# Graph layer with edge sums on one core: the last four groups counted in advance, and their first places sent through DRAM as a 123rd row of the rank product

## Chip, core and metric

The kernel runs on 1 core of one Trainium2 chip. The metric is the device time of an execution in microseconds (us); lower is better. Engines are called PE or TensorE (matrix products), DVE or VectorE, ACT or ScalarE, POOL or GpSimd (here it issues the indirect transfers) and SP or SyncE (here it issues nearly all direct transfers).

## What is computed

```python
def _L0_gnn_ref(x, edge_index, edge_features, ...):
    row = edge_index[0]                                   # the source node of each edge
    edge_aggr = jnp.zeros((n, 128)).at[row].add(edge_features)
    combined = jnp.concatenate([x, edge_aggr, global_expand], axis=-1) @ W_c + b_c
    h = jax.nn.softplus(combined @ W1 + b1)
    h = jax.nn.softplus(h @ W2 + b2)
    return h @ W3 + b3
x = _layernorm(x + _L0_gnn_ref(...), axis=-1)
```

There are 6,250 nodes and 206,250 edges, each with 128 float32 features (106 MB). `src` holds the source node of each edge in no order. Nearly all work is in the second line: the features of the edges are added up by source node. The matrix products of the layer that follows are small.

## The kernel before

**Layout.** The edges stand as 1,692 columns of 122 rows (`PN`). Two columns are a *pair*, so there are 846 pairs, which fall into eight *groups* of 28, 72, 124, 124, 124, 128, 124 and 122 pairs. The nodes are cut into 32 *buckets* of 196 (`BL`). The kernel sorts the edges by bucket, through DRAM, and then sums each bucket with matrix products.

**Sorting a pair.** ScalarE or VectorE builds a one-hot of each edge's place in its pair (*compare*: `sort_hot`, L1139 on VectorE, L1142 and L1144 on ScalarE); TensorE multiplies the edges' rows by it (*gather*: `sorted`, L1155); ScalarE copies the sorted rows into one of six buffers (*settle*: `pairs`, L1167); POOL issues one indirect transfer per pair, which writes the rows to their buckets in DRAM (*scatter*: `rows_by`, L1184). Compare, gather and settle are done for three pairs at a time, a piece. Of the pairs, a share of three in five is compared by VectorE.

**Summing.** SP loads chunks of a bucket back (`chunks<-rows_by`, L293, in six buffers), VectorE makes a one-hot of the node within the bucket (*match*: `hot`, L990), TensorE multiplies (*product*: `part`, L1013), VectorE adds the parts up (*add*: `sums_t`, L1036). A chunk may be loaded once enough columns have been scattered that its rows are certainly there. The planner works this out from sizes of buckets and adds the visits to the order. The chunks of the *last column* become certain only after the last scatter. Then the node layers follow. Room that no edge fills has to be zero, so 23 fill transfers (`rows_by<-fill`) write zeros ahead.

**Positions.** Before a group can be sorted, its positions must be known. Per group: `node_codes` (twelve VectorE operations over the whole group, L357 to L393) gives each edge its bucket; then, per set of 16 columns, `count_set` makes a one-hot of the buckets (`pair_ib`, 122 rows by 512, L498) and `counted` multiplies it by ones (L509). Per batch of four sets VectorE keeps the even counts (L520), TensorE turns them into first places of runs by products with triangular matrices (L527), and VectorE stores these (`started`: L534, L536, and a bfloat16 copy `starts_h`, L538) and handles odd counts (`odd_set`, L546 to L551). Scans over the group end the counting pass. A second pass ranks the edges: per set one product of the rank matrix with `pair_ib` (`ranked`, L557), to which four products with an identity add the first places (L559), and VectorE picks the slot of each edge (L576). Then come the pair tables (L727, L742, L753 to L764).

**The order.** The whole order of instructions is written by a planner: every step gets a due time from modelled durations (1.3 us a scatter), the steps are sorted by time and issued, and each engine then runs its instructions in that order as soon as their inputs are there. The steps for later groups' positions are spread evenly over 0.85 of the time of the group that is being scattered. For groups up to `GAP`, both passes are done in the time of the group ahead. From `GAP` = 5 on, groups are *split*: the counting pass is done early, and the second pass, which makes the one-hots again, in the time of the group ahead. Once the counts of all groups are known, room in the buckets is dealt out exactly: groups before `GAP` fill their buckets from the front, groups from `GAP` on from the end. Fills are due ahead of group `GAP`'s first column.

| scattered meanwhile | positions work before the change |
|---|---|
| group 2 | group 3 whole, count of group 5 |
| group 3 | group 4 whole, count of group 6 |
| group 4 | count of group 7, second pass of group 5 |
| groups 5, 6 | second pass of group 6, of group 7 |

Of the kernel before, what the change touches and what calls it, by code (L numbers as in the profile page):

```python
# [18 lines left out]
P = 128  # L19
# [14 lines left out]
GAP = 5  # L34
# [36 lines left out]
APART = 3  # L71
# [32 lines left out]
def tables_of(n_buckets):  # L104
# [31 lines left out]
    t["rank"] = MARK * (k == f) + (f > k)  # L136
# [10 lines left out]
def kernel(  # L147
# [35 lines left out]
    assert 2 * BATCH * STEP + SPAN <= 4 * P and BATCH * STEP // QUAD + SPAN <= P  # L183
# [98 lines left out]
    totals = dram.tile([N + 2, D], F32, name="totals")  # L282

# [35 lines left out]
    with ExitStack() as phase:  # L319
# [25 lines left out]
        rank_h = rank_h[:PN, :PN]  # L345
# [5 lines left out]
        def scratch(name):  # L351
            return per.tile([P, 4 * P], F32, name=name, bufs=1)
# [98 lines left out]
        def positions(g):  # L451
# [22 lines left out]
            def opened():  # L474
                if sets:
                    if not split:
                        opened2()
                    own["odd"] = per.tile([KB, 2, Q_MAX], BF16, name="odd", bufs=1)
                    own["evens"] = per.tile([KB, Q_MAX], BF16, name="evens", bufs=1)
                    own["alone"] = per.tile([KB, Q_MAX], BF16, name="alone", bufs=1)  # L480
                    late, deep = ("_late", G - GAP) if split else ("", 1)
                    own["starts"] = per.tile([KB, 2, Q_MAX], F32, name="starts" + late, bufs=max(2, deep))
                    own["starts_h"] = per.tile([KB, Q_MAX], BF16, name="starts_h" + late, bufs=deep)
                    own["earlier"] = per.tile([KB, 2, Q_MAX], F32, name="earlier" + late, bufs=deep)
# [7 lines left out]
            def count_set(t):  # L492
                n = size(t)
                m = n // QUAD
                ib = pairs_in.tile([PN, STEP // QUAD, SB, QUAD], BF16, name="pair_ib", bufs=5)[:, :m]
                in_set[t] = ib
                cols = pair_block[:, 2 * s0 + t:2 * s0 + t + n].rearrange("p (q c) -> p q c", c=QUAD)
                nc.vector.tensor_tensor(  # L498
                    ib, cols.unsqueeze(2).to_broadcast([PN, m, SB, QUAD]),
                    bucket_at[:PN].unsqueeze(1).to_broadcast([PN, m, SB, QUAD]),  # L500
                    op=ALU.is_equal)

            def counted(ts):
                small = whole(small_bank())
                small_of["counts", ts] = small
                for t in ts:
                    for q in range(per_set(t)):
# [3 lines left out]
                            in_set[t][:, q].rearrange("p b c -> p (b c)"),  # L511
# [11 lines left out]
            def evened(ts):  # L523
                at = quads_of(ts)
                n = at.stop - at.start
                for k, by in enumerate((lower_h, through_h, lower_or_all_h)):
                    nc.tensor.matmul(small_of["counts", ts][:KB, (1 + k) * P:(1 + k) * P + n], by,  # L527
                                     own["evens"][:, at], start=True, stop=True)

            def started(ts):  # L530
                at = quads_of(ts)
                n = at.stop - at.start
                small = small_of["counts", ts][:KB].rearrange("k (a q) -> k a q", a=4)
# [4 lines left out]
                nc.vector.tensor_copy(own["starts_h"][:, at], small[:, 1, :n])  # L538

            def odd_set(ts):  # L540
                at = quads_of(ts)
                n = at.stop - at.start
                small = small_of.pop(("counts", ts))[:KB].rearrange("k (a q) -> k a q", a=4)
# [9 lines left out]
            def ranked(t):  # L553
# [3 lines left out]
                nc.tensor.matmul(pr, rank_h, in_set.pop(t)[:, :, :NB, :], start=True, stop=False)  # L557
# [270 lines left out]
            else:  # L828
# [367 lines left out]
        with tc.manual_schedule(engines={ET.PE, ET.DVE, ET.Activation, ET.SP}):  # L1196
# [111 lines left out]
            ahead_of[G - 1], position_steps = [], {}  # L1308
# [310 lines left out]
```

## Time and profile before

| | before |
|---|---|
| median of 3 runs | 1282.51 us (1279.74 to 1284.93) |
| the profiled execution | 1280.91 us |
| span of its trace | 1279.1 us |
| busy: PE, its weight loads, DVE, ACT, POOL | 1156.0, 1098.4, 1047.0, 913.4, 883.6 us |
| granted TensorE clock, mean | 0.972 |

The span runs from the first to the last recorded instruction; the execution is 1.8 us longer. Rows of the trace give the start in us, the duration in us, the engine, the line in the code, the operation, what is written from what, and the shape of a tile; x4 says that four instructions are taken together; brackets give the idle time ahead of the row and what ended it. Rows with the releaser "issue" waited for nothing that the profile shows. The line numbers are those of the kernel before; in the changed kernel most stand about 25 lines lower (compare L1164, gather L1180, product L1038, add L1061, one-hot L501, SP's transfers L295).

### The profile page before, as it was taken

How to read it: one execution, taken by the hardware profiler on the slowest of the kernel's cores; microseconds unless marked ns; L12 is line 12 of the kernel's file. 1: busy time of each engine (PE TensorE's matmuls, PEld its weight loads, DVE VectorE, ACT ScalarE, POOL GpSimd, SP SyncE). 2: the span in 40 equal slices, each digit the busy share in tenths (PEclk: the TensorE clock that was granted, in tenths of full speed). 3: DMA queues.
4: the chain of work that ended last, by engine and by line, in shares of the span. 5: the costliest groups of instructions: out<-in, count | busy, mean ns of one | idle time of the engine just before them, and what ended most of it. 6: DMA issues, size and time to landing. Idle time of an engine off the chain costs nothing.

```text
span 1279.1 us, 26170 instructions
## 1 busy us (share of the span) xinstructions
PE 1156.0 (90%) x8617; PEld 1098.4 (86%) x8617; DVE 1047.0 (82%) x2289; ACT 913.4 (71%) x2150; POOL 883.6 (69%) x915
## 2 busy tenths in 40 slices
PE   5777898797998899989899999999999999899893
PEld 4677788787998898989899999999999999898772
DVE  7878979986789898899888887789877767687784
ACT  5887877886776688866987878877888888303343
POOL 2777777776777777777777777777777777750334
PEclk9988999998899899999999999999999999999996
DMA  6789999999999989997999999999999999875421
GB/s 242 249 304 357 334 314 306 346 340 334 338 347 331 333 315 336 322 315 266 320 317 312 313 340 329 337 319 332 322 350 335 363 343 355 286 234 144 142 69 54
DMA packets 174635, 381.95 MB, mean 299 GB/s; under 512 B 27546, under 2 KB 118626, under 8 KB 160670
## 3 DMA queue, kind: packets, MB, share of 16 engines
q1 hardware_dynamic: 130751, 260.70, 61.7%
q0 software_dynamic: 41328, 115.65, 23.3%
q10 hardware_dynamic: 2415, 3.85, 0.8%
q8 instruction: 72, 1.18, 0.4%
q14 instruction: 69, 0.57, 0.1%
HBM read 242.47 MB, written 142.20 MB: 301 GB/s over the span
## 4 chain that ended last, share of the span: by engine, by line
PE 62%; DVE 11%; DMA 11%; ACT 6%; issue 5%; POOL 4%; SPq 0%; ACTq 0%; DVEq 0%; POOLq 0%
PE part L1013 37%; PE sorted L1155 20%; DMA rows_by<-pairs,pair 7%; POOL rows_by L1184 4%; ACT pairs L1167 3%; DMA chunks<-rows_by 3%; DVE hot L990 2%; ACT sort_hot L1142 1%; PE small L557 1%; PE small L559 1%; DVE past L727 1%; DVE sort_hot L1139 1%; PE small L1397 1%; PE sorted L1362 1%; DVE slot L576 1%
## 5 line engine op out<-in xcount | busy, mean ns | idle before, releaser
L1184 POOL DMA_INDIRECT rows_by<-pairs,pair x846 | 830.5, 982 | 289.3 <-issue 208.1
L1167 ACT COPY pairs<-sorted 64x387 f32<-64x387 f32 (+2 forms) x1144 | 543.5, 475 | 224.0 <-PE sorted L1155 165.1
L1013 PE MATMUL part<-hot,chunks 128*128 128x196 f32 x3516 | 671.0, 334 | 16.0 <-DVE sums_t L1036 9.0
L1013 PEld LDWEIGHTS part<-hot,chunks 128*128 128x128 f32 x3516 | 577.4, 191 | 25.2 <-DVE sums_t L1036 10.7
L1155 PE MATMUL sorted<-rows,sort_hot 122*128 122x129 f32 x3384 | 489.6, 284 | 36.3 <-ACT pairs L1167 25.3
L1155 PEld LDWEIGHTS sorted<-rows,sort_hot 122*128 122x128 f32 x3384 | 448.9, 196 | 45.7 <-ACT pairs L1167 35.7
L990 DVE TENSOR_TENSOR hot<-chunks,both_ps 128x784 f32<-128x784 f32 (+3 forms) x541 | 427.1, 810 | 11.7 <-DMA chunks<-rows_by 7.7
L1036 DVE TENSOR_TENSOR sums_t<-sums_t,part 128x392 f32<-128x392 f32 (+1 forms) x262 | 143.6, 548 | 115.9 <-PE part L1013 113.0
L1142 ACT ACTIVATE sort_hot<-plain,slot 122x128 f32<-122x128 f32 x684 | 227.9, 392 | 8.8 <-DVE slot L576 5.9
L1139 DVE TENSOR_TENSOR sort_hot<-slot,both_ps 122x768 f32<-122x768 f32 (+2 forms) x172 | 159.6, 928 | 7.7 <-PE sorted L1155 7.4
L1144 ACT ACTIVATE sort_hot<-sort_hot 122x768 f32<-122x768 f32 x114 | 95.9, 841 | 0.2
L1439 POOL TENSOR_SCALAR y<-y,mv,rs 128x128 f32<-128x128 f32 x40 | 31.3, 788 | 91.1 <-DVE rs L1427 90.8
L576 DVE TENSOR_REDUCE slot<-small 122x16 f32<-122x512 f32 (+2 forms) x109 | 72.9, 669 | 16.5 <-PE small L559 16.0
L498 DVE TENSOR_TENSOR pair_ib<-pair_block,plain 122x512 bf16<-122x512 bf16 (+2 forms) x157 | 63.5, 411 | 0.2
L1369 ACT ACTIVATE away<-sorted,z_bias 128x512 f32<-128x512 f32 (+2 forms) x13 | 8.5, 656 | 71.8 <-DMA chunks<-rows_by 46.4
L557 PE MATMUL small<-pair_ib,half 122*122 122x512 bf16 (+2 forms) x109 | 42.6, 391 | 9.9 <-DVE slot L576 9.6
L742 PEld LDWEIGHTS <-past 128*128 128x128 f16 x424 | 24.7, 98 | 22.6 <-DVE past L727 17.8
L742 PE MATMUL small<-jump,past 128*128 128x56 f16 (+3 forms) x424 | 28.8, 188 | 16.3 <-DVE past L727 12.1
L727 DVE TENSOR_TENSOR past<-both_ps,starts 128x512 f16<-128x512 f32 (+1 forms) x61 | 39.7, 666 | 0.2
L559 PEld LDWEIGHTS <-starts_h 128*122 128x122 bf16 x236 | 24.9, 146 | 13.2 <-issue 8.7
L727 DVE TENSOR_TENSOR past<-both_ps,starts_late 128x512 f16<-128x512 f32 (+2 forms) x49 | 32.4, 662 | 0.0
L1116 ACT COPY rows<-pair_i 122x16 f32<-122x16 f32 x106 | 22.3, 211 | 7.8 <-DMA rows<-in_edge 6.9
(161 smaller groups left out, 516.7 us busy)
## 6 DMA issues: line engine op xcount, KB each, us to landing
rows<-in_edge SPq DMA_DIRECT2D x105, 1032.0 KB
chunks<-rows_by SPq DMA_DIRECT2D x362, 136.0 KB
chunks<-rows_by SPq DMA_DIRECT2D x203, 204.0 KB
chunks<-rows_by SPq DMA_DIRECT2D x75, 272.0 KB
rows_by<-pairs,pair POOLq DMA_INDIRECT x846
rows_by<-fill SPq DMA_DIRECT2D x10, 1249.5 KB
rows_by<-fill SPq DMA_DIRECT2D x10, 714.0 KB
chunks<-rows_by SPq DMA_DIRECT2D x13, 408.0 KB
```

Of the source, the lines that this page charges most:

```text
L498: nc.vector.tensor_tensor(ib, cols.unsqueeze(2).to_broadcast([PN, m, SB, QUAD]), bucket_at[:PN].unsqueeze(1).to_broadcast([PN, m, SB, QUAD ...
L576: nc.vector.tensor_reduce(to, of, axis=mybir.AxisListType.X, op=ALU.max)
L727: nc.vector.tensor_tensor(past[:, :, a:b], twice_ps[:KB].unsqueeze(1).unsqueeze(1).to_broadcast([KB, 2, b - a, P // 2]), own["starts"][:, ...
L990: nc.vector.tensor_tensor(hot[:, q - a:q - a + m], chunks[j][:, lo:hi + 1:step, D:W].to_broadcast([P, m, BL]), iota_ps.unsqueeze(1).to_bro ...
L1013: nc.tensor.matmul(part[:, b - base_of[v], :], t[:, place_in(j, q), :D], hot[:, q - a], start=first, stop=last)
L1036: nc.vector.tensor_add(here, here, of)
L1139: return [lambda: nc.vector.tensor_tensor(hot[:PN, :2 * m], slot[:PN, at:at + 2 * m].unsqueeze(2).to_broadcast([PN, 2 * m, P]), slot_ps[:P ...
L1142: return [lambda j=j: nc.scalar.activation(hot[:PN, j], by_slot[:PN], AF.Abs, bias=slot[:PN, at + j:at + j + 1], scale=-1.0) for j in rang ...
L1144: for j in range(2 * m)] + [lambda: nc.scalar.activation(hot[:PN, :2 * m], hot[:PN, :2 * m], AF.Relu, bias=1.0, scale=-1.0)]
L1155: nc.tensor.matmul(out[:, j, :], hot[:PN, at], rows_at[col // LOAD_COLS][:PN, col % LOAD_COLS, :], start=True, stop=True)
L1167: nc.scalar.copy(sets_at[i][64 * n:64 * n + 64, lo:lo + m, h, :W], out[64 * h:64 * h + 64, :m, :])
L1184: s = nc.gpsimd.indirect_dma_start(out=dst, out_offset=bass.IndirectOffsetOnAxis(ap=at, axis=0), in_=rows[:, j].rearrange("p a b -> p (a b ...
```

## The change

`GAP` becomes 4, so that group 4 is split too, and a table says in which group's time each split group is counted: 4 and 5 in group 2's, 6 and 7 in group 3's.

| scattered meanwhile | positions work after the change |
|---|---|
| group 2 | group 3 whole, counts of groups 4 and 5 |
| group 3 | counts of groups 6 and 7, second pass of group 4 |
| group 4 | second pass of group 5 |
| groups 5, 6 | second pass of group 6, of group 7 |

In split groups the four L559 products per set go. The rank matrix gets a 123rd row of ones, and the one-hot tile a 123rd row that holds the first places of the set. For this, a further product per batch gives the first places turned round (a set's positions in rows), VectorE casts them (`starts_rows`, in place of the `starts_h` cast), SP writes them to DRAM (16 transfers in all), and SP reads for each set of the second pass 512 values of them into row 123 of the one-hot (64 transfers of 1 KB). The rank product of a set comes 13 steps after its one-hot and its row's transfer (`ROW_LEAD`), where it was 3.

```diff
-GAP = 5
+GAP, COUNTED_IN = 4, {4: 2, 5: 2, 6: 3, 7: 3}
-APART = 3
+APART, ROW_LEAD = 3, 13
-    t["rank"] = MARK * (k == f) + (f > k)
+    t["rank"] = MARK * (k == f) + (f > k) + (k == PN)
...
+    rows_of = {g: dram.tile([2 * (s1 - s0) // QUAD, KB], BF16, name=f"starts{g}")
+               for g, (s0, s1) in enumerate(groups) if g >= GAP}
...
-                ib = pairs_in.tile([PN, STEP // QUAD, SB, QUAD], BF16, name="pair_ib", bufs=5)[:, :m]
+                ib = pairs_in.tile([PN + 1, STEP // QUAD, SB, QUAD], BF16, name="pair_ib", bufs=5)[:, :m]
...
+                if split:
+                    nc.tensor.matmul(small_of["counts", ts][:n, P:P + KB], own["evens"][:, at],
+                                     lower_h, start=True, stop=True)
...
-                nc.vector.tensor_copy(own["starts_h"][:, at], small[:, 1, :n])
+                if not split:
+                    nc.vector.tensor_copy(own["starts_h"][:, at], small[:, 1, :n])
+                    return
+                rows_h = per.tile([BATCH * STEP // QUAD, KB], BF16, name="starts_rows", bufs=2)
+                nc.vector.tensor_copy(rows_h[:n], small_of["counts", ts][:n, P:P + KB])
+                sync_dma(rows_of[g][at], rows_h[:n])
+
+            def starts_row(t):
+                q0, n = t // QUAD, per_set(t)
+                sync_dma(in_set[t][PN:PN + 1].rearrange("p q b c -> p (q b c)"),
+                         rows_of[g][q0:q0 + n].rearrange("(o q) k -> o (q k)", o=1))
...
-                nc.tensor.matmul(pr, rank_h, in_set.pop(t)[:, :, :NB, :], start=True, stop=False)
+                k = PN + split
+                nc.tensor.matmul(pr, rank_h[:k], in_set.pop(t)[:k, :, :NB, :], start=True, stop=split)
+                if split:
+                    return
                 for q in range(per_set(t)):
...
                     at_step(4 * n, (6, lambda t=t: count_set(t)))
-                    rank(n, 4 * n + APART, t)
+                    at_step(4 * n, (7, lambda t=t: starts_row(t)))
+                    rank(n, 4 * n + ROW_LEAD, t)
...
-            ahead_of = {g: [(g + 1, 0)] for g in range(G - 1)}
-            ahead_of[GAP - 1] = [(GAP, 1)]
+            ahead_of, position_steps = {g: [(g + 1, 0)] if g + 1 < GAP else [] for g in range(G)}, {}
+            for k, g in COUNTED_IN.items():
+                ahead_of[g].append((k, 0))
             for k in range(GAP, G):
-                ahead_of[k - 3].insert(-1 if k == G - 1 else 1, (k, 0))
-            for k in range(GAP + 1, G):
-                ahead_of[k - 1] = [(k, 1)]
+                ahead_of[k - 1].append((k, 1))
```

Three places show how the order of instructions moves. The first is VectorE in group 2's time, from one comparison (`sort_hot`) to the next; the second of the two comparisons is that for pair 208. Before:

```order
L1139 TENSOR_TENSOR sort_hot<-slot,both_ps 122x768
L498 TENSOR_TENSOR pair_ib<-pair_block,plain 122x512
L1036 TENSOR_TENSOR sums_t<-sums_t,part 128x392
L498 TENSOR_TENSOR pair_ib<-pair_block,plain 122x512
L520 TENSOR_SCALAR evens<-small 128x16
L1139 TENSOR_TENSOR sort_hot<-slot,both_ps 122x768
```

After, at the same place:

```order
L1164 TENSOR_TENSOR sort_hot<-slot,both_ps 122x768
L523 TENSOR_SCALAR evens<-small 128x16
L501 TENSOR_TENSOR pair_ib<-pair_block,plain 122x512
L1061 TENSOR_TENSOR sums_t<-sums_t,part 128x392
L545 TENSOR_SCALAR starts_late<-small 128x16
L547 TENSOR_SCALAR starts_late<-small,plain 128x16
L553 CAST starts_rows<-small 16x128
L501 TENSOR_TENSOR pair_ib<-pair_block,plain 122x512
L1164 TENSOR_TENSOR sort_hot<-slot,both_ps 122x768
```

The steps of the counting passes stand closer together between the comparisons, since three passes share the stretch that two had; all of group 4's counting now stands ahead of this place. The second place is SP in group 3's time, where chunk loads and the loads of edge rows (`rows<-in_edge`) stand. Before:

```order
L293 DMA chunks<-rows_by 128x408
L293 DMA chunks<-rows_by 128x272
L293 DMA chunks<-rows_by 128x408 x2
L293 DMA chunks<-rows_by 128x272 x11
L293 DMA rows<-in_edge 128x2064 x3
```

After, a visit of the same form, in which the transfers of group 4's first places (named `starts_79` there) stand before, between and behind:

```order
L295 DMA pair_ib<-starts_79 1x512
L295 DMA chunks<-rows_by 128x408
L295 DMA chunks<-rows_by 128x272
L295 DMA chunks<-rows_by 128x408 x2
L295 DMA chunks<-rows_by 128x272 x11
L295 DMA pair_ib<-starts_79 1x512 x2
L295 DMA rows<-in_edge 128x2064
L295 DMA pair_ib<-starts_79 1x512 x4
L295 DMA rows<-in_edge 128x2064
L295 DMA pair_ib<-starts_79 1x512 x5
```

Chunk loads now stand in SP's queue behind transfers that wait for VectorE or for TensorE. The third place is TensorE at the end of the sorting, around the last gather (`sorted<-rows,sort_hot`) up to the first product of the node layers (`x_t,fold`). Before:

```order
L1155 MATMUL sorted<-rows,sort_hot 128x129 x2
L1013 MATMUL part<-hot,chunks 128x196 x4
L1155 MATMUL sorted<-rows,sort_hot 128x129 x2
L1013 MATMUL part<-hot,chunks 128x196 x19
L1293 MATMUL small<-most_of,ones 1x48
L1013 MATMUL part<-hot,chunks 128x196 x101
L1358 MATMUL sorted<-x_t,fold 128x512
```

After:

```order
L1180 MATMUL sorted<-rows,sort_hot 128x129 x2
L1038 MATMUL part<-hot,chunks 128x196 x4
L1180 MATMUL sorted<-rows,sort_hot 128x129 x2
L1038 MATMUL part<-hot,chunks 128x196 x21
L1318 MATMUL small<-most_of,ones 1x48
L1038 MATMUL part<-hot,chunks 128x196 x52
L1381 MATMUL sorted<-x_t,fold 128x512
```

Behind the last gather stand 73 products up to the node layers instead of 120; 47 have moved ahead of it, since with four groups placed exactly more chunks are certain earlier.

More of the change, by code (lines that the diff above doesn't have):

```diff
@@ L351, in scratch @@
         def scratch(name):
-            return per.tile([P, 4 * P], F32, name=name, bufs=1)
+            return per.tile([P, 2 * B_MAX], F32, name=name, bufs=1)
         def whole_nodes(part, n):
@@ L482, in opened @@
                     own["starts"] = per.tile([KB, 2, Q_MAX], F32, name="starts" + late, bufs=max(2, deep))
-                    own["starts_h"] = per.tile([KB, Q_MAX], BF16, name="starts_h" + late, bufs=deep)
+                    if not split:
+                        own["starts_h"] = per.tile([KB, Q_MAX], BF16, name="starts_h", bufs=1)
                     own["earlier"] = per.tile([KB, 2, Q_MAX], F32, name="earlier" + late, bufs=deep)
@@ L532, in started @@
                 n = at.stop - at.start
-                small = small_of["counts", ts][:KB].rearrange("k (a q) -> k a q", a=4)
+                small = by_kind(small_of["counts", ts])
                 nc.vector.tensor_scalar(own["starts"][:, 0, at], small[:, 1, :n], 0.0, None,
```

18 lines of the change are left out of this document (11 added, 7 removed).

## The prediction

> **What bounds the kernel now.** I read the page first: busy shares, the chain that ended last, the costliest groups.
>
> ```profile
> span 1279.1 us, 26170 instructions
> PE 1156.0 (90%) x8617; PEld 1098.4 (86%) x8617; DVE 1047.0 (82%) x2289; ACT 913.4 (71%) x2150; POOL 883.6 (69%) x915
> PE 62%; DVE 11%; DMA 11%; ACT 6%; issue 5%; POOL 4%; SPq 0%; ACTq 0%; DVEq 0%; POOLq 0%
> L1184 POOL DMA_INDIRECT rows_by<-pairs,pair x846 | 830.5, 982 | 289.3 <-issue 208.1
> ```
>
> TensorE is the busiest and carries 62% of the chain; this would make it the bound. But the fourth row is a metronome: 846 scatters whose idle time is mostly "issue", which waits for nothing shown. So I took the timeline of POOL next: the first scatter, those of pairs 208, 320 and 444, and the last two.
>
> ```profile
> 22.52 1.23 POOL L1184 DMA_INDIRECT rows_by<-pairs,pair  x1 [20.89 <-DVE much L646]
> ...
> 292.50 0.97 POOL L1184 DMA_INDIRECT rows_by<-pairs,pair  x1 [0.30 <-issue]
> ...
> 446.44 1.18 POOL L1184 DMA_INDIRECT rows_by<-pairs,pair  x1 [0.30 <-issue]
> ...
> 606.70 0.97 POOL L1184 DMA_INDIRECT rows_by<-pairs,pair  x1 [0.51 <-ACT pairs L1167]
> ...
> 1119.21 0.98 POOL L1184 DMA_INDIRECT rows_by<-pairs,pair  x1 [0.30 <-issue]
> 1120.49 0.97 POOL L1184 DMA_INDIRECT rows_by<-pairs,pair  x1 [0.30 <-issue]
> ```
>
> Undisturbed, a scatter starts 1.28 us after the one before it (last two rows). From first to last there are 845 steps in 1098.0 us; at 1.28 they would take 1082, so all engines together cost POOL only 16 us before 1121. The scatter phase is POOL's issue rate plus those 16 us. Where they fall, and what else has room, is in the windows (columns: length, then busy time of PE, PEld, DVE, ACT, POOL, the granted TensorE clock, the DMA share, GB/s).
>
> ```profile
> 141.00:292.00 151.00, 129.84 (x1077) 122.47 (x1077) 132.33 (x330) 118.28 (x282) 114.84 (x117) 0.97 0.94 329
> 292.00:356.00 64.00, 56.68 (x397) 54.16 (x396) 44.73 (x89) 45.03 (x109) 44.47 (x46) 0.89 0.96 338
> 356.00:464.00 108.00, 98.48 (x816) 94.69 (x815) 98.89 (x241) 77.26 (x185) 79.21 (x81) 0.97 0.96 339
> 807.00:1121.00 314.00, 308.25 (x2240) 304.89 (x2239) 244.57 (x386) 237.22 (x565) 239.36 (x246) 1.00 0.96 333
> 1121.00:1279.00 158.00, 129.43 (x669) 107.64 (x668) 116.36 (x284) 52.85 (x95) 52.42 (x65) 0.93 0.41 126
> ```
>
> From pair 208 to 320 POOL took 153.9 us where 112 steps ask for 143.4: 10.5 of the 16 are lost there. In the fourth window, 98% busy TensorE costs POOL nothing: 246 scatters times 1.28 are 314.9, its whole length. A full TensorE alone does not stop the scatters while it keeps its lead. The last row is the tail: 158 us after the last scatter, TensorE busy for 129.
>
> POOL's waits name its suppliers: the first three rows are 153 to 317 us, the next two 317 to 483, the last 643 to 1121 (columns: total, times, longest).
>
> ```profile
> POOL rows_by L1184 <- issue: 30.2, 99, 0.4
> POOL rows_by L1184 <- DMA rows_by<-pairs,pair: 8.6, 13, 3.2
> POOL rows_by L1184 <- ACT pairs L1167: 2.2, 7, 0.4
> ...
> POOL rows_by L1184 <- DMA rows_by<-pairs,pair: 7.0, 14, 1.2
> POOL rows_by L1184 <- ACT pairs L1167: 4.7, 7, 1.9
> ...
> POOL rows_by L1184 <- ACT pairs L1167: 7.6, 25, 0.3
> ```
>
> Waits of 0.3 are the usual gap. Longer ones are of two kinds, both between 153 and 483: earlier scatters that land late (longest 3.2), and pairs not settled yet (1.9). The second is what extra work on VectorE or TensorE would lengthen, since a pair is compared, gathered, settled and then scattered.
>
> **The change, part by part.**
>
> *1. Products leave the path.* The order of instructions has 249 fewer products of line 559 and 16 more, which turn the first places.
>
> ```profile
> 863.59 0.39 PE L559 MATMUL small<-half,starts_h_late 128*122 128x128 bf16 x4
> 863.82 0.88 PE L1013 MATMUL part<-hot,chunks 128*128 128x196 f32 x4
> ```
>
> Four hold TensorE until the next row starts: 0.23 us, 57 ns each. 249 give 14.2 us; 16 more of at most that price cost 0.9. This -13.3 lies beside the scatters, where TensorE had its lead: nothing at the end by itself.
>
> *2. A counting pass comes into group 2's time.* Group 4 is now counted beside groups 3 and 5: 368 steps instead of 285 are spread over 137 us (0.85 of 124 pairs at the planner's 1.3), and VectorE must do them ahead of the comparisons of this stretch.
>
> ```profile
> 425.54 0.45 DVE L357 CAST first<-pair_i 122x248 f32<-122x248 int32 x1
> ...
> 430.64 1.09 DVE L498 TENSOR_TENSOR pair_ib<-pair_block,plain 122x512 bf16<-122x512 bf16 x3
> ...
> 443.86 0.18 DVE L546 CAST odd_i<-small 128x32 int32<-128x32 f32 x1
> ...
> 444.87 0.42 DVE L498 TENSOR_TENSOR pair_ib<-pair_block,plain 122x512 bf16<-122x512 bf16 x1
> ```
>
> Node codes take from 425.54 to 430.64, 5.1 us; a one-hot is 0.335 of VectorE's time, 16 of them 5.4; the odd counts take 1.01 per batch, and with first places and even counts (0.4, estimated from the odd counts' five instructions) 1.4, so 5.6 for four batches; scans and the pass's end some 4 by the same estimate. A counting pass is 20 us. The order puts that much more VectorE work ahead of the comparisons of pairs 208 to 266 (+20), then +24 at pair 326, +32 at 341 where the counts of groups 6 and 7 and the second pass of group 4 meet, +17 at 444.
>
> What of it shows? Comparisons run well ahead:
>
> ```profile
> 274.64 0.94 DVE L1139 TENSOR_TENSOR sort_hot<-slot,both_ps 122x768 f32<-122x768 f32 x1
> ...
> 597.88 0.94 DVE L1139 TENSOR_TENSOR sort_hot<-slot,both_ps 122x768 f32<-122x768 f32 x1
> ```
>
> These compare pairs 208 and 444: 17.9 and 8.8 us before their scatters at 292.50 and 606.70. The latter waited just 0.51, so some 9 us are enough and pair 208 has 9.1 to give. VectorE's idle time is 18.7 us in 141:292, but waits in order can't all be filled; I take half, 9.4. Then 20 - 9.4 = 10.6 us late against 9.1: **+1.5**. At pair 341 another 12 come; half of the 9.1 idle in 356:464 covers 4.5, and 1.5 of lead is left: **+6**. If no idle time can be filled, 20.3 - 9.1 and 12 - 1.5 cost 11.2 + 10.5 = 22; if all can, nothing. The scatters can't win time lost, as they step at 1.28 at best.
>
> *3. Transfers.* 16 rows of first places go out and 64 return; both stand in SP's queue among chunk loads, and a write waits for VectorE, a read from the sixth on for TensorE to free the one-hot's buffer. The chunk loads behind them feed the sums, which are not POOL's suppliers. What the bytes cost is nothing (64 KB against 330 GB/s). The same 23 fills, however, are due by pair 348 and no more by 472:
>
> ```profile
> rows_by<-fill SPq DMA_DIRECT2D x10, 1249.5 KB
> rows_by<-fill SPq DMA_DIRECT2D x10, 714.0 KB
> ```
>
> These 20 are 19.6 MB, spread over 386 us instead of 547 (the due dates at 1.3 us a pair, less the planner's slack). So 17% of them, 3.4 MB, come forward across 483 us: 10 us at 330 GB/s, into windows whose DMA share of 0.94 to 0.96 leaves 5%, some 16 us. POOL waited longest there for its own scatters' landing. Between 0 (all fits) and 10 (nothing does) I take **+2**, near to nothing because a share of 0.96 in 807:1121 cost POOL nothing.
>
> *4. The rank's row must be there in time.* 13 steps are 23 us in groups 4 to 6 and 7.3 us in group 3, whose 243 steps are spread over 137 us. If a row is late, TensorE stands at the rank product, with all gathers behind it. Landings to go by are these:
>
> ```profile
> 96.96 13.43 DMA chunks<-rows_by
> ...
> 948.92 2.93 DMA rows_by<-pairs,pair
> ```
>
> From 2.9 to 13.4 us; a single KB is nearer to the short one: 0.
>
> *5. The tail.* Chunks become certain earlier, so 47 products move ahead of the last gather: behind it stand 240 instead of 287, 44 instead of 91 of them ahead of the 196 of the last column.
>
> ```profile
> 1101.64 0.61 PE L1155 MATMUL sorted<-rows,sort_hot 122*128 122x129 f32 x4
> 1102.09 6.47 PE L1013 MATMUL part<-hot,chunks 128*128 128x196 f32 x38
> ...
> 1120.21 27.39 PE L1013 MATMUL part<-hot,chunks 128*128 128x196 f32 x162 [3.12 <-DVE sums_t L1036]
> ...
> 1130.13 98.78 SPq L293 DMA_DIRECT2D chunks<-rows_by  x71
> ```
>
> A product leaves two records: 162 in 27.39 us are 0.34 each, so 47 are 15.7. But not all comes back. 39 products are done before 1120.21, the other 52 last until 1137.5, and there the last column's begin; it can't begin before the last scatter has landed (1121.5 + 2.9) and its chunk is loaded and matched (4 to 8 more): 1128 to 1132. So 5 to 9, **-7**, with 0 and -15.7 as ends: nothing, if loads and VectorE set the tail.
>
> **Sum.** The profiled execution is 1280.9, its span 1279.1 and 1.8 around it. +1.5 + 6 + 2 + 0 - 7 = +2.5, which makes 1283.4. The median of the runs shown, 1282.5, is 1.6 above the profiled one: 1285.0.
>
> **The rivals.** Measured from no change, 0.5% (6.4 us) is about what can be told.
>
> *R1, VectorE has no usable idle time.* Comparisons fall behind by the whole counting pass, POOL waits for pairs from pair 208 on. For it: most of VectorE's idle time stands ahead of one instruction, the sums' addition, which waits for products of TensorE's; what is behind it in order can't use the time.
>
> ```profile
> L1036 DVE TENSOR_TENSOR sums_t<-sums_t,part 128x392 f32<-128x392 f32 (+1 forms) x262 | 143.6, 548 | 115.9 <-PE part L1013 113.0
> ```
>
> Against it: in 292:356 VectorE is idle for 19.3 of 64 us and is to get only 12 more. It is decided if POOL waits for settled pairs for over 15 us before 483. Price: 22 (the transfers' 2 would hide in the same waits) - 7 = 15: 1297.5. Slower.
>
> *R2, TensorE is the bound.* Then its -13.3 comes off: 1269. For it: 90% busy and 62% of the chain. Against it: 98% busy at 807:1121 with POOL in full step. The Trainium skill, "Perfetto Trace Analysis", section "Identifying the Most-Contended Engine", says to optimise the engine with the highest occupancy first, and to judge TensorE by the time of its weight loads; here these are 86%, above VectorE's 82, and by the rule this rival would be the forecast. The scatters' step is why I don't follow it.
>
> *R3, VectorE's idle time takes it all.* 18.7 + 19.3 (292:356) + 9.1 of idle time exceed 32. Then +1 for transfers and a tail of -9: 1274.5. Faster.
>
> *R4, the row lands late in group 3's time*, like the 13.4 us load against 7.3: 6 us once, for all gathers behind it: 1291. Slower.
>
> **Chances.** Forecast 0.42 (its own range 1278 to 1290), R1 0.25, R3 0.15, R2 0.10, R4 0.08. Faster by over 0.5%: R3 and R2, 0.25; slower: R1 and R4, 0.33; within: 0.42. The range reaches from between R2 and R3, 1271, to just above R1, 1298.
>
> **What would show it.** VectorE's busy time up by some 20 us before 292 and 12 by 356; POOL's loss up by 5 to 12 us between pairs 208 and 444 as waits for settled pairs, none new later; 57 ns per product gone from TensorE, with no wait for a transfer at a rank; 44 products ahead of the last column's, which begins 7 us earlier against the last scatter. The forecast is wrong if POOL's loss stays at 16 us (R3), doubles (R1), or if the tail doesn't shrink.

## The result, and the profile after

The changed kernel takes 1297.64 us, median of 5 runs (1294.96 to 1299.30), against 1279.74 us before (5 runs, 1277.79 to 1284.93): a ratio of 1.0132, 95% interval 1.0105 to 1.0159. It is slower, by 1.3%. Its profiled execution took 1294.96 us, that of before 1280.91. The two traces can account for these 14.05 us; the medians lie 17.9 apart.

The page's first rows, the chain by engine and the scatters:

```profile
span 1293.2 us, 25809 instructions
PE 1147.5 (89%) x8384; PEld 1090.4 (84%) x8384; DVE 1053.6 (81%) x2301; ACT 912.6 (71%) x2150; POOL 881.7 (68%) x915
...
PE 47%; DVE 16%; DMA 16%; POOL 9%; issue 7%; ACT 5%; ACTq 0%; POOLq 0%; DVEq 0%; SPq 0%
...
L1209 POOL DMA_INDIRECT rows_by<-pairs,pair x846 | 828.9, 980 | 313.1 <-issue 206.5
```

TensorE is busy for 8.5 us less, VectorE for 6.6 more, and the span is 14.1 longer. POOL's idle time went from 289.3 to 313.1. Its timeline says where; the rows are the first scatter, those of pairs 195 and 196, those of pairs 208 and 348, and the last. Behind them stands the scatter of pair 348 in the kernel before:

```profile
22.75 1.22 POOL L1209 DMA_INDIRECT rows_by<-pairs,pair  x1 [21.12 <-DVE much L670]
...
285.29 0.97 POOL L1209 DMA_INDIRECT rows_by<-pairs,pair  x1 [0.31 <-issue]
293.45 0.97 POOL L1209 DMA_INDIRECT rows_by<-pairs,pair  x1 [7.19 <-ACT pairs L1192]
...
311.86 0.97 POOL L1209 DMA_INDIRECT rows_by<-pairs,pair  x1 [0.30 <-DMA rows_by<-pairs,pair]
...
505.71 0.97 POOL L1209 DMA_INDIRECT rows_by<-pairs,pair  x1 [0.30 <-DMA rows_by<-pairs,pair]
...
1142.70 0.97 POOL L1209 DMA_INDIRECT rows_by<-pairs,pair  x1 [0.30 <-issue]
...
483.02 0.97 POOL L1184 DMA_INDIRECT rows_by<-pairs,pair  x1 [0.30 <-ACT pairs L1167]
```

From the first to the last scatter are 1119.95 us, 21.98 more than before. Measured against the undisturbed step (1.281 us), POOL had lost 3.5 us at pair 208 and 14.7 at pair 348 before; now it is 22.7 and 37.2. From pair 348 on it loses nothing in either kernel: 637.0 us now, 637.5 before. What is left of the span behind the start of the last scatter is 150.5 us, where it was 158.6. So the 14.1 us between the two spans are some +22 in the first 348 pairs and -8.1 in the tail.

POOL's waits for settled pairs and for its own scatters' landing, first in 150 to 500 us after, then in 150 to 480 before (total, times, longest):

```profile
POOL rows_by L1209 <- ACT pairs L1192: 36.6, 25, 7.2
POOL rows_by L1209 <- DMA rows_by<-pairs,pair: 9.6, 23, 1.1
...
POOL rows_by L1184 <- DMA rows_by<-pairs,pair: 15.6, 27, 3.2
POOL rows_by L1184 <- ACT pairs L1167: 6.9, 14, 1.9
```

The waits for pairs took 29.7 us more, the waits for landings 6.0 less. ScalarE, which settles the pairs, waited 29.9 us for landings to free a buffer between 150 and 500 us before, and 1.3 now: it no longer runs ahead of POOL. Why the pairs are late shows at the comparison of pair 208:

```profile
302.38 0.94 DVE L1164 TENSOR_TENSOR sort_hot<-slot,both_ps 122x768 f32<-122x768 f32 x1
```

Before, it started at 274.64: it comes 27.7 us later, and 9.5 us ahead of its scatter, where it was 17.9 ahead. From the first scatter to this row VectorE is busy for 236.0 of 279.6 us; in the same stretch before it was 218.3 of 252.1. So there are 17.7 us more work, and 9.8 us more idle time on top of it. Of the idle time, 5.6 us are matches that wait for chunk loads (3.45 us at 115.17 and 3.74 at 202.78, against one wait of 1.59). Both of these waits come before the first write of first places, at 256.1.

The windows of after (columns as before) show what the suppliers did, the last four around two of the places where POOL lost time:

```profile
141.00:292.00 151.00, 119.88 (x987) 113.18 (x987) 131.10 (x342) 102.85 (x246) 102.84 (x105) 0.89 0.96 332
292.00:356.00 64.00, 57.28 (x482) 55.36 (x481) 55.54 (x143) 53.58 (x130) 45.79 (x47) 1.00 0.84 302
356.00:464.00 108.00, 95.16 (x748) 91.30 (x747) 99.26 (x270) 72.72 (x174) 76.42 (x79) 0.95 0.78 272
...
250.00:273.00 23.00, 20.49 (x201) 19.43 (x201) 18.88 (x59) 18.11 (x45) 15.43 (x16) 1.00 0.99 328
273.00:291.00 18.00, 9.74 (x46) 9.37 (x46) 15.62 (x51) 8.34 (x20) 10.21 (x11) 0.53 0.87 324
291.00:312.00 21.00, 18.00 (x187) 16.93 (x184) 17.69 (x55) 14.03 (x36) 12.16 (x13) 1.00 0.55 199
...
430.00:470.00 40.00, 30.58 (x226) 27.96 (x225) 38.71 (x111) 23.36 (x56) 22.97 (x25) 0.96 0.63 217
```

In 141 to 292 us VectorE is as busy as before (131.1 against 132.3) although 20 us more stood ahead of the comparisons: its idle time was not filled, the work behind was put off, and POOL has 105 instructions there where it had 117. In 292 to 356 us it is busy for 10.8 us more than before. In 430 to 470 us it has next to no idle time to fill: it is busy for 38.7 of 40.

The largest loss, the 7.19 us at 293.45, can be followed back. VectorE's rows:

```profile
262.51 0.93 DVE L1164 TENSOR_TENSOR sort_hot<-slot,both_ps 122x768 f32<-122x768 f32 x1
...
272.72 0.28 DVE L553 CAST starts_rows<-small 14x128 bf16<-14x128 f32 x1 [1.65 <-DMA starts<-starts_rows]
272.92 0.93 DVE L1164 TENSOR_TENSOR sort_hot<-slot,both_ps 122x768 f32<-122x768 f32 x1
...
275.51 0.28 DVE L619 TENSOR_TENSOR_SCAN total_late<-enough,small 128x62 f32<-128x62 f32 x1 [0.46 <-PE small L610]
...
279.35 0.48 DVE L359 CAST first<-pair_i 122x256 f32<-122x256 int32 x1
...
284.50 0.42 DVE L501 TENSOR_TENSOR pair_ib<-pair_block,plain 122x512 bf16<-122x512 bf16 x1
284.85 1.44 DVE L1015 TENSOR_TENSOR hot<-chunks,both_ps 128x588 f32<-128x588 f32 x2
```

and TensorE's in the same time:

```profile
275.11 0.26 PE L610 MATMUL small<-alone,half 128*128 128x62 bf16 x2 [3.52 <-DVE alone L572]
...
285.66 1.35 PE L1038 MATMUL part<-hot,chunks 128*128 128x196 f32 x3 [6.16 <-DVE hot L1015]
```

From 273.8 to 284.8 us VectorE does group 4's last odd counts and scans and then at once group 5's bucket codes: no comparison and no match between 272.92 and 284.85. TensorE runs out of work twice, for 3.52 us from 271.59 on and for 6.16 us from 279.50 on, its granted clock in that window is 0.53, and the gathers behind the product at 285.66 come late: this product waits for a match that stands behind the block. The change brought the second piece of that block next to the first, since group 5 is now counted right behind group 4.

One wait is of the change's own making: the cast at 272.72 stood 1.65 us for a free buffer, because of this write of 4 KB, which the chain of waits shows:

```profile
262.28 10.42 DMA starts<-starts_rows
```

The cast's wait (271.07 to 272.72) falls for the most part into TensorE's wait of 3.52 us, so some 1.1 us of this first wait belong to the transfers and not to the block.

The tail, from SP (the last column's loads) and TensorE:

```profile
1145.70 98.19 SPq L295 DMA_DIRECT2D chunks<-rows_by  x71
...
1124.49 7.13 PE L1038 MATMUL part<-hot,chunks 128*128 128x196 f32 x42
1131.56 0.25 PE L1318 MATMUL small<-most_of,ones 128*1 128x48 f32 x2
1131.73 7.90 PE L1038 MATMUL part<-hot,chunks 128*128 128x196 f32 x46
1149.58 12.23 PE L1038 MATMUL part<-hot,chunks 128*128 128x196 f32 x58 [9.96 <-DVE hot L1015]
```

The 44 products ahead of the last column's (88 records) are done at 1139.6, three us before the last scatter starts. The first load is issued 3.0 us after that start, and the last column's products begin 6.9 us after it, behind 10 us of an idle TensorE; before it was 17.3 us (1137.82; the prediction had 1137.5). That is the other end of the same trade: the start of the last column is now set by landing, loading and matching, no more by products.

The rank product finds its row in place:

```profile
884.93 0.38 PE L579 MATMUL small<-pair_ib,half 123*122 123x512 bf16 x1
885.15 0.83 PE L1180 MATMUL sorted<-rows,sort_hot 122*128 122x129 f32 x6
```

0.22 us to the next row, where rank and four additions took 0.44. In the whole trace the waits of the rank products are for VectorE (L600, 16.1 us in all); none is for a transfer.

### The profile page after: what moved, and what is told of

Its sections match the earlier page's. It is cut to its first block, busy times and chain, and to the rows that moved or that the text cites. A ratio compares the mean times of both kernels' runs of the same rounds, so it can differ in the third digit from the quotient of the medians.

```text
span 1293.2 us, 25809 instructions
## 1 busy us (share of the span) xinstructions
PE 1147.5 (89%) x8384; PEld 1090.4 (84%) x8384; DVE 1053.6 (81%) x2301; ACT 912.6 (71%) x2150; POOL 881.7 (68%) x915
## 4 chain that ended last, share of the span: by engine, by line
PE 47%; DVE 16%; DMA 16%; POOL 9%; issue 7%; ACT 5%; ACTq 0%; POOLq 0%; DVEq 0%; SPq 0%
PE part L1038 27%; PE sorted L1180 15%; DMA rows_by<-pairs,pair 11%; POOL rows_by L1209 9%; DMA chunks<-rows_by 3%; DVE hot L1015 3%; ACT pairs L1192 2%; DVE slot L600 1%; DVE past L751 1%; DVE sort_hot L1164 1%; ACT sort_hot L1167 1%; DVE sums_t L1061 1%; PE small L579 1%; DVE pair_ib L501 1%; PE small L1420 1%
## 5 line engine op out<-in xcount | busy, mean ns | idle before, releaser
L1209 POOL DMA_INDIRECT rows_by<-pairs,pair x846 | 828.9, 980 | 313.1 <-issue 206.5
L1180 PEld LDWEIGHTS sorted<-rows,sort_hot 122*128 122x128 f32 x3384 | 452.9, 197 | 46.9 <-ACT pairs L1192 36.6
L600 DVE TENSOR_REDUCE slot<-small 122x16 f32<-122x512 f32 (+2 forms) x109 | 72.7, 667 | 13.6 <-PE small L583 12.6
L501 DVE TENSOR_TENSOR pair_ib<-pair_block,plain 122x512 bf16<-122x512 bf16 (+2 forms) x173 | 69.7, 409 | 0.2
L579 PE MATMUL small<-pair_ib,half 123*122 123x512 bf16 (+4 forms) x109 | 43.2, 396 | 16.1 <-DVE slot L600 16.1
L766 PEld LDWEIGHTS <-past 128*128 128x128 f16 x424 | 24.8, 99 | 22.6 <-DVE past L751 14.7
L751 DVE TENSOR_TENSOR past<-both_ps,starts_late 128x512 f16<-128x512 f32 (+1 forms) x65 | 42.8, 660 | 0.0
L583 PEld LDWEIGHTS <-starts_h 128*122 128x122 bf16 x174 | 19.1, 151 | 14.6 <-issue 11.7
L751 DVE TENSOR_TENSOR past<-both_ps,starts 128x512 f16<-128x512 f32 (+1 forms) x45 | 29.1, 664 | 0.8 <-PE small L766 0.6
L512 PE MATMUL small<-ones_h,pair_ib 122*128 122x48 bf16 x423 | 17.9, 187 | 12.5 <-DVE pair_ib L501 12.2
```

The lines of the kernel that those rows point to most:

```text
L501: nc.vector.tensor_tensor(ib[:PN], cols.unsqueeze(2).to_broadcast([PN, m, SB, QUAD]), bucket_at[:PN].unsqueeze(1).to_broadcast([PN, m, SB, ...
L600: nc.vector.tensor_reduce(to, of, axis=mybir.AxisListType.X, op=ALU.max)
L751: nc.vector.tensor_tensor(past[:, :, a:b], twice_ps[:KB].unsqueeze(1).unsqueeze(1).to_broadcast([KB, 2, b - a, P // 2]), own["starts"][:, ...
L1180: nc.tensor.matmul(out[:, j, :], hot[:PN, at], rows_at[col // LOAD_COLS][:PN, col % LOAD_COLS, :], start=True, stop=True)
L1209: s = nc.gpsimd.indirect_dma_start(out=dst, out_offset=bass.IndirectOffsetOnAxis(ap=at, axis=0), in_=rows[:, j].rearrange("p a b -> p (a b ...
```

## The experiments

Theories: A, the added counting pass itself, VectorE work ahead of comparisons; B, the transfers of first places in SP's queue; C, the fills that come forward; D, not the amount of VectorE work but its blocks; T, TensorE's load.

All of them fell on chips on which the kernel before takes 1591 to 1631 us. With all products, TensorE's granted clock is 0.88 to 0.91 in these runs, it stands in many waits for which the trace shows no releaser, and POOL waits for pairs all along (342.8 us in the first experiment); the runs do not show why. So each kernel is compared only with kernels on the same chip, and none shows POOL at its own step. The changed kernel itself was not run on these chips with all its products. How different they are, a window over each whole span shows, of before in the first comparison and of the first experiment:

```profile
0.00:1279.00 1279.00, 1156.03 (x8617) 1098.44 (x8617) 1046.99 (x2289) 913.38 (x2150) 883.59 (x915) 0.97 0.86 299
...
0.00:1629.00 1629.00, 1300.75 (x8442) 1197.70 (x8442) 1049.98 (x2289) 912.28 (x2150) 881.26 (x915) 0.89 0.70 235
```

**Four kernels on one chip.** Rows without the counts:

```diff
-GAP, COUNTED_IN = 4, {4: 2, 5: 2, 6: 3, 7: 3}
+GAP, COUNTED_IN = 5, {5: 2, 6: 3, 7: 4}
```

> The changed kernel with five groups placed as before (GAP 5) and counted where they were before (5 in group 2's time, 6 in 3's, 7 in 4's); only the first places of groups 5 to 7 still come by DRAM as the 123rd row, asked for 13 steps ahead. Theory A (the added counting pass fills VectorE ahead of the comparisons): nothing is counted earlier, so POOL loses 15 to 18 us as before and the time is within 4 us of before. Theory B (the transfers of first places hold chunk loads in SP's queue, and VectorE waits for these in order): POOL loses 5 to 10 us more wherever rows are written, time 1285 to 1290. A TensorE that sets the time would give some 10 us less than before.

The counts without the rows (the changed kernel, with these taken back and the four L559 products per set in their place):

```diff
...
-                    at_step(4 * n, (7, lambda t=t: starts_row(t)))
-                    rank(n, 4 * n + ROW_LEAD, t)
+                    rank(n, 4 * n + APART, t)
```

> The changed kernel's groups and counts (GAP 4, groups 4 and 5 counted in group 2's time, 6 and 7 in 3's), but with the first places added by the four products per set as before, 3 steps after the one-hot: no row goes through DRAM. Theory A: as slow as the changed kernel, 1294 to 1300, POOL loses 35 to 42 us, the tail stays 8 us shorter. Theory B: without the transfers POOL's loss falls to 22 to 28 us, 1283 to 1288.

The kernel before with early fills:

```diff
-            done_by = FIRST + SCATTER * todo[-1][0] - SLACK
+            done_by = FIRST + SCATTER * (todo[-1][0] - 124) - SLACK
```

> The kernel before with its 23 fills spread over the time up to 416 us, as in the changed kernel, where they were spread up to some 577; nothing else differs. If the fills that come forward fill the transfer engines (Theory C), POOL loses 5 to 10 us more between 150 and 420 us, waiting for its own scatters, 1284 to 1290. By Theory A it is within 3 us of before.

The changed kernel with the bucket codes as single steps (`code_steps` gives the operations of `node_codes` one by one):

```diff
...
-                        prep += [lambda k=k: node_codes(k)]
+                        codes = code_steps(k)
                         position_steps[k] = positions(k)
+                        if len(prep) > 60:
+                            at = len(prep) - 52
+                            for j, step in enumerate(codes):
+                                prep.insert(at + 5 * j, step)
+                        else:
+                            prep += codes
```

> The changed kernel with the twelve operations that give a group's edges their buckets spread between the last 60 steps of the group counted before, where they stood in one block of 5 us behind the 4 us of scans. Same work. If the amount of VectorE work costs the time (Theory A), within 4 us of the changed kernel, 1293 to 1300. If it is the blocks, during which neither comparison nor match is done (Theory D), POOL's loss falls by 6 to 12 us, 1286 to 1291.

Measured against the kernel before on that chip (1621.23 us, 31 runs; the others 10 runs each):

| kernel | median us | ratio, 95% interval |
|---|---|---|
| rows, GAP 5 | 1618.89 | 0.9989 (0.9952 to 1.0025) |
| GAP 4, products | 1623.11 | 1.0039 (0.9994 to 1.0083) |
| early fills | 1620.67 | 0.9979 (0.9946 to 1.0012) |
| codes spread | 1618.21 | 0.9965 (0.9932 to 0.9997) |

No expected time came true; they were written for a kernel before of 1280. Of the expectations relative to before, two of Theory A held: rows, GAP 5 lies 2.3 us below it (within 4 was expected) and early fills 0.6 (within 3). What can be said: the rows alone cost nothing that shows there (by the interval between 7.8 us less and 4.1 more), which speaks against B on these chips, and also against T, by which they should have saved some 10 us. Early fills cost nothing there either, but their DMA share was 0.83 in 141 to 292 us and 0.72 in 292 to 483, so this is no test of C, whose point was a share of 0.95.

**Two of them again, on a second chip,** where the kernel before takes 1600.63 us (6 runs):

> The same kernel as in the run with GAP 4 and the four products, looked at again where POOL's step sets the time, as in the first comparison, and not TensorE's own issuing. Theory A (the counting pass): as slow as the changed kernel, 1293 to 1300, POOL loses 35 to 42 us. Theory B (the transfers of first places): POOL loses 22 to 28 us, 1283 to 1288.

> The same kernel as in the run with the bucket operations spread out, again where POOL's step sets the time. Theory A: the amount of work counts, 1293 to 1300. Theory D (the blocks): POOL's loss falls by 6 to 12 us, 1286 to 1291.

GAP 4 with products took 1586.13 (ratio 0.9957, 0.9887 to 1.0027), codes spread with rows 1579.56 (0.9858, 0.9779 to 0.9938). On both chips the kernel with rows and without the products is below the one with them, by 5 and 7 us; the intervals overlap. It is too little to tell the missing products from the spread codes. Codes spread is the one kernel whose interval lies below 1 on both chips, on the second with two runs.

**One run each, on a third and a fourth chip:**

> GAP 4 with the four products per set, a third look, for its profile. Where the kernel before takes some 1280: Theory A (the counting pass on VectorE) 1293 to 1300 with a POOL loss of 35 to 42 us; Theory B (the transfers of first places) 1283 to 1288 with a loss of 22 to 28. Where the kernel before takes some 1600, TensorE's own issuing sets the time (Theory T): then this kernel is within 1% of before, and 12 to 16 us above a kernel without the 249 products.

1628.49 us, beside 1630.62 of before: within the 1% that T expected.

> GAP 5, counted as before, with the first places of groups 5 to 7 by DRAM: a second look. Where the kernel before takes some 1280: Theory A (the counting pass) within 4 us of it and a POOL loss of 15 to 18 us; Theory B (the transfers) 5 to 10 us more of both. Where the kernel before takes some 1600 and TensorE's issuing sets the time (Theory T): some 10 us less than it, for 187 products less.

1593.85, beside 1591.56 of before. 187 products less gave no 10 us, but these are single runs, and ten runs of this kernel on the first chip lay up to 24 us apart; the weight against T is in those ten.

**Four kernels with products left out, on a fifth chip.** To bring POOL's step back as the bound, TensorE was relieved:

```diff
-                    nc.tensor.matmul(part[:, b - base_of[v], :], t[:, place_in(j, q), :D], hot[:, q - a],
-                                     start=first, stop=last)
+                    if first or col == NC:
+                        nc.tensor.matmul(part[:, b - base_of[v], :], t[:, place_in(j, q), :D], hot[:, q - a],
+                                         start=first, stop=last or col != NC)
```

> The kernel before with 1082 of its 1758 products of chunks left out (of each bucket only the first in a visit, all of the last column), so that TensorE has some 360 us less to do and POOL's step sets the time even where TensorE issues slowly; matches, loads, additions, comparisons, gathers and scatters are all there, the sums are not those of the reference. All theories: POOL at its own step, loss 10 to 40 us, time 1230 to 1300: it is the measure for the next three.

> The changed kernel with the same products left out. Theories A (counting work on VectorE), B (transfers of first places) and D (blocks of VectorE work) all expect POOL to lose 12 to 25 us more up to pair 348 than the kernel before with the same cut. If TensorE's fullness was needed for the loss (Theory T), it loses less than 6 us more, and the time is not above that of the cut kernel before.

> GAP 4 and the early counts, first places added by the four products, the same products of chunks left out. Theory A: POOL loses as much up to pair 348 as the cut changed kernel, within 4 us. Theory B: 8 us less or more, near the cut kernel before.

> The changed kernel with the bucket operations spread out between the steps of the group counted before, the same products of chunks left out. Theory A: POOL's loss up to pair 348 is within 4 us of the cut changed kernel. Theory D: it is 6 to 12 us less.

The kernel before takes 1595.53 us there (4 runs). With the cut (2 runs each) before takes 1555.96 (1548.04 to 1563.88), the changed one 1541.55 (1531.96 to 1551.15), GAP 4 with products 1547.33 (1546.14 to 1548.52), codes spread 1547.97 (1543.03 to 1552.91). The aim was missed: some 360 us of products were gone, and the time fell by 40. POOL still waited for pairs, so the first expectation (1230 to 1300) failed. The whole span of the cut kernel before:

```profile
0.00:1546.00 1546.00, 1024.56 (x6453) 900.19 (x6453) 1044.40 (x2289) 912.21 (x2150) 881.40 (x915) 0.80 0.73 247
```

The traces say something of A, B and D, though little. The scatters of pairs 0 and 348 of the cut before, the cut changed kernel, the cut GAP 4 with products, and the cut codes spread:

```profile
22.70 1.22 POOL L1185 DMA_INDIRECT rows_by<-pairs,pair  x1 [21.07 <-DVE much L646]
...
588.27 0.97 POOL L1185 DMA_INDIRECT rows_by<-pairs,pair  x1 [0.30 <-issue]
...
22.87 1.22 POOL L1210 DMA_INDIRECT rows_by<-pairs,pair  x1 [21.24 <-DVE much L670]
...
599.73 0.97 POOL L1210 DMA_INDIRECT rows_by<-pairs,pair  x1 [0.30 <-issue]
...
22.49 1.23 POOL L1195 DMA_INDIRECT rows_by<-pairs,pair  x1 [20.85 <-DVE much L656]
...
604.97 0.97 POOL L1195 DMA_INDIRECT rows_by<-pairs,pair  x1 [2.83 <-ACT pairs L1178]
...
23.23 1.22 POOL L1265 DMA_INDIRECT rows_by<-pairs,pair  x1 [21.60 <-DVE much L725]
...
607.77 0.97 POOL L1265 DMA_INDIRECT rows_by<-pairs,pair  x1 [4.53 <-ACT pairs L1248]
```

The first 348 pairs take 565.6, 576.9, 582.5 and 584.5 us. The three kernels that count group 4 early need 11, 17 and 19 us more than the one that does not (12 to 25 was expected of the first of them), with rows or without, with codes in a block or spread. Behind the last scatter's start all three need 155 to 156 us, the cut kernel before 169. B expected a lower time up to pair 348 without the transfers, D with the codes spread; neither is lower. But the differences of 5.6 and 7.7 us to the cut changed kernel are not within A's 4 us either.

This points to the early count and does not show it. These are single profiles. That of the cut before is of the faster of its two executions, those of the other three are of the slower ones, and by the medians all three are faster than the cut before, by 8 to 14 us; of the two things that T expected, less than 6 us more up to pair 348 and a time not above the cut before, the second is so. On these chips one and the same kernel's time from pair 0 to 348 differs by up to 29 us (GAP 4 with products, three chips). The uncut kernels of the first chip point the same way, as weakly: 603.7 us (rows, GAP 5) and 594.6 (early fills) without the early count, 613.4 (GAP 4, products) and 606.4 (codes spread) with it.

The tail is clearer. In all twelve traces of these chips the span behind the last scatter's start is 155 to 158 us with GAP 4, with rows or with products, and 169 to 174 with GAP 5.

No version came out that beats both kernels where POOL sets the time; none could be tried there.

## Why the prediction was right or wrong

The measured 1297.6 lies in the range, at its upper end, but the likeliest case, 1285.0, did not come true. What came true is the rival R1, to which 0.25 was given and a price of 1297.5.

*The step that failed* is part 2's "I take half, 9.4": that VectorE's idle time would take half of the added work. Its terms were +1.5 and +6; the scatters lost 22.0 us more, near the price of no idle time used at all. The criterion set for it was over 15 us of waits for settled pairs before 483 us; they were 20.2 from 150 to 312 us and 36.6 up to 500. The comparison of pair 208, forecast 10.6 us late, came 27.7 late: 17.7 us of added work (20 was estimated), and idle time that did not shrink but grew by 9.8. Why the idle time was no use is visible: idle pieces are waits for TensorE's products and for loads in the middle of VectorE's order, while the added work came in blocks (11 us at 273.8) and into stretches with hardly a hole (430 to 470 us). What the idle time in a window is worth depends on whether the work behind the added work is what POOL waits for.

That the price of R1 was met to 0.1 us is luck. It counted from 1282.5, where the median of before is 1279.74 with five runs: R1 priced a rise of 15 us, and the medians rose by 17.9, the profiled executions by 14.05. Within the trace, R1 put 11.2 us at pair 208, from a comparison 20.3 late, and 10.5 at pair 341. The trace has 19.1 more by pair 208, from a comparison 27.7 late, 1.9 less than before from there to pair 320, and 5.3 more to pair 348. The sum was right and its parts were not. The slack of 9.1 us that the prediction read from one comparison was there: 8.4 of it were used, and 9.5 us of lead were enough. But POOL lost its time before pair 208 already: 4.9 us between 165 and 200 us in waits that are not for pairs, and from 230 us on in waits for pairs, the longest from the block at 273.

*Part 1* held: a rank is 0.22 us shorter, the 249 products are gone, and nothing of it shows in the time. TensorE's busy time fell by 8.5 us and not by 13.3; products and gathers took 2.4 us more, at a mean clock of 0.961 against 0.972, and the rest is not traced. R2, TensorE as the bound, was wrong: its work fell and the time rose. So the Trainium skill's rule ("Perfetto Trace Analysis", "Identifying the Most-Contended Engine"), by which the busiest engine is to be optimised first, would have led astray for this change; the step of the scatters was the better sign.

*Part 3*, +2 for fills: the waits for landings fell by 6.0 us in total, as POOL stood for pairs instead. Some 4.9 us were lost between 165 and 200 us, with a DMA share of 1.02 in 160 to 190, in waits for landings of about 1 us and one of 2.08 for issue. That fits the fills that come forward: 15 of the 23 are issued before 200 us, where there were 10. Matches then waited 7.2 us for chunk loads ahead of pair 208's comparison, against 1.6, and VectorE works in order, so the comparisons behind stood too. The part's view that chunk loads are not POOL's suppliers missed this. Whether the fills caused these waits stays open, since no run tested it at that share.

*Part 4*, nothing for late rows: held; R4 was wrong, and so was R3, which needed the idle time to be of use. What the part missed is the other direction, VectorE waiting for a row's write to leave its buffer (1.65 us once). SP's queue does stand behind VectorE now: 34.1 us in seven waits between 150 and 305 us, the longest 15.5, where the like came to 1.2, and the DMA share fell to 0.55 in 291 to 312, from 0.91. But from the first write at 256.1 to 500 us no match waits for a chunk load and no compare or gather for edge rows, so the 1.65 us are all that the traces show of a cost of these transfers up to there.

*Part 5*, the tail: -7 forecast, -8.1 measured, for the reason given (products moved ahead, and from then on landing, load and match). The last column's products begin 10.4 us earlier against the last scatter, where 7 was forecast; 8.1 of this reached the end.

What the runs settle: that the loss is waits for settled pairs, behind comparisons that VectorE makes later, with 17.7 us more work and 9.8 more idle time ahead of pair 208 (traces of before and after); and that the shorter tail comes with GAP 4. That the rows' transfers have little part in the loss follows from the trace of after (1.65 us of waits up to 500 us); the runs on the other chips agree with it. What stays open: how the 22 us divide between the counting pass, its blocks and the fills that come forward. No run takes one of them away where POOL sets the time.

## What to carry to other kernels

Idle time of an engine that works in order is not room: before work is added, look at what the idle pieces wait for and which instruction of the critical supplier will stand behind the addition; with no such reading, price the added work in full. Here even that was too little: 17.7 us of work made a comparison 27.7 us late. Where one engine steps at a fixed rate, count its lost steps by place; this located both the loss and the absence of a gain better than busy shares did. Work that is spread evenly by steps is not spread evenly by time: two steps of 4 and 5 us next to each other made a block behind which TensorE ran out of work.

## What the runs showed of the hardware

TensorE's granted clock fell while TensorE waited. The windows lie around the waits of 3.52 us (from 271.59) and 6.16 us (from 279.50), the last one behind a wait of 1.85 us that ended at 160.64:

```profile
272.00:274.00 2.00, 0.00 (x0) 0.00 (x0) 1.25 (x4) 1.94 (x6) 1.39 (x2) 0.90 1.00 389
274.00:276.00 2.00, 0.90 (x7) 0.89 (x7) 1.40 (x6) 0.74 (x2) 1.52 (x2) 0.50 1.03 391
...
288.00:290.00 2.00, 2.00 (x9) 2.00 (x9) 1.91 (x4) 0.67 (x2) 0.00 (x0) 0.50 0.23 91
290.00:292.00 2.00, 2.00 (x26) 1.93 (x26) 0.95 (x2) 1.03 (x2) 0.00 (x0) 0.84 0.05 15
...
162.00:164.00 2.00, 2.00 (x21) 1.82 (x21) 2.00 (x4) 1.96 (x6) 1.39 (x3) 0.50 1.02 293
```

The clock is 0.50 from 274 to 290 us and was 1.00 in 250 to 273. Eighteen gathers at 275.28 took 4.22 us in it, where twelve at 267.20 took 1.61. The Trainium skill says in "TensorE: Matmul & The Clock Gate", section "What's actually happening", that the clock falls to half after an idle window of about 3.4 us. The trace agrees on the half, but not on 3.4 us as the least length of a wait: the clock fell less than 2.5 us into the first wait, and after the wait of 1.85 us it was 0.50 as well. So a late supplier costs twice here, by the wait and by the slower work behind it.

In the cut kernel before, with TensorE busy for 66% of the span, the mean clock was 0.80; the kernel before had 0.89 to 0.91 on that chip. Some 360 us of products were taken away, and TensorE got the rest at a lower clock.

An undisturbed indirect scatter is issued every 1.28 us in both kernels (0.97 and 0.30 between), while a 4 KB write at 262.28 us needed 10.42 us to land at a DMA share of 0.99.
